# Gated cross-attention with a mixture of experts: the first group's steps issued ahead of all others

## The chip, the core and the metric

The kernel runs on one core of a Trainium2 chip. The time is device time in microseconds for one execution; the median over several runs is compared. The core has a matrix engine (PE), a vector engine (DVE), a scalar engine (ACT), a general engine (POOL) and a queue engine that mostly starts transfers (SP). ACT and POOL can start transfers too. Each engine takes its instructions in order; the engines wait for one another through semaphores.

## The reference, cut to what matters

```python
# x (64, 128, 128), context (64, 77, 96), mask (64, 77)
x = x + tanh(g_xattn[0]) * attention(layernorm(x), context, mask, Wq, Wk, Wv, Wo)
x = x + tanh(g_ffn[0]) * moe(layernorm(x), Wg, W11, W12, W2)

# attention: 16 heads of 8
q, k, v = x @ Wq, context @ Wk, context @ Wv          # split by heads
scores = where(mask, q @ k.T * 8**-0.5, -max)         # 128 x 77 for each head
out = (softmax(scores) @ v) @ Wo

# moe: 8 experts, the 2 best for each token
top, idx = top_k(softmax(x @ Wg), 2); top = top / (top.sum(-1) + 1e-8)
out = sum over the two of top * ((silu(x @ W11[e]) * (x @ W12[e])) @ W2[e])
```

All arrays are float32 but the mask.

## The kernel before, in words

**Tiling.** The 64 batches of 128 tokens are 16 groups of four (`G = 4`, `NG = 16`). A group has a tile of x (128 partitions x 4 x 128, 256 KB) that stays on the chip, a tile of context (77 x 4 x 96) and, in the attention part, keys, queries and values of its own. After the attention, tokens are sent by expert to a buffer in HBM in two parts (groups 0 to 11, and 12 to 15), worked on there in tiles of 128 rows, and brought back, added to x and stored.

**The mask.** `keep64` holds it as 64 x 77 numbers (L216). It is used in three ways: transposed by PE to `keepT`, from which `firstT` (the first kept position of each batch) and `drop` (what is added to a score's exponent) come; as `live` (L246), which zeroes the layer norm's factor of a batch with no position kept; and by rows: it is stored to `keep_d` in HBM (L218) and each group loads its four rows back, copied to all 77 partitions, as `kr` (L456). POOL makes from it a selection matrix `sel` (steps `sel_0`, `sel_1`, `sel_2`, L479 to L499) with which the context is multiplied while it is transposed.

**The steps of a group.** The attention of a group is cut into named steps: `loads` (x, context and `kr` on SP), `stats_a0` and `stats_a1` (mean and variance on DVE, then Ln and Exp on ACT and the product with `live` on POOL, L342 to L355), `shift_a` (L359, DVE), `rows_a0` and `rows_a1` (the normalized rows, ACT, L365), `queries_t` (four transposes on PE and a copy on ACT, `pt`), `queries` (`pq`, L543), `context_t` (`pc`, L505), `keys` (`pk`, L526, and four scaled copies `kb` on ACT, L532). Then come the batches, one in each turn: `scores` (`sc`, L840, four PE products; then on DVE the maximum `mx`, L849, and two differences `pe` and `pls`, L852), `turn` (eight transposes `tp`, L862, and exponentials on ACT, L867), `turn_last` (`tl`, L875), `values` (`pv`, L813 and L825, and a copy `va` on ACT, L831), `mix` (48 products `po`, L894). Later steps of the group (`inverses`, `quotients`, `project`, `residual` and the routing) follow some turns on.

**The order.** Inside the block that contains the attention the order on PE, ACT, DVE and POOL is the order in which the program issues the instructions; SP's loads stand in the order of the program and of their buffers. A table `AT` gives each step a turn relative to its group's first batch and whether it stands before (`PRE`) or after (`POST`) the turn's batch work. The main loop (L916) counts turns from -15; `advance` issues, in each half turn, the steps of all groups that fall due, so in the turns ahead of batch 0 the steps of groups 0, 1, 2 and 3 alternate. In turn i the scores of batch i, the transposes of batch i-1, the values of batch i+2 and the product of batch i-2 are issued.

**Buffers.** The scores have one PSUM tile of four banks (`ps_sc`), so a batch's scores wait for DVE to have read the last batch's. All other products share three PSUM tiles (`product`, L372): transposes, queries, keys, `po` and `tl` in turn. `values` writes one PSUM tile `pv`, read by `va`. Four context tiles and three `kr` tiles are in turn, so a later load waits until an earlier tile has been read. A transfer also waits for the transfer eight before it to have landed, since eight semaphores are used in turn.

**The start.** SP starts the mask and the context of group 0, ACT the x of group 0, then Wk, Wq, Wv, eight pieces of Wo (rows are permuted on the way, L129), Wg and the two gates (L133, L134). ACT makes `tg`, the tanh of the gates, with a table of its own, and then loads the table of Ln and Exp (L305, L307); DVE makes `wo` from `tg` and `wo_in` (L306) and then takes up the statistics.

Of the kernel before, what the change touches and what calls it, by code (L numbers as in the profile page):

```python
# [8 lines left out]
F32 = mybir.dt.float32  # L9
# [4 lines left out]
ALU = mybir.AluOpType  # L14
# [5 lines left out]
NQ = 4  # L20
HQ = HEADS // NQ
G = 4
# [14 lines left out]
def tile_gated_xattn_moe(  # L37
# [81 lines left out]
    nc.sync.dma_start(out=mask_u8, in_=mask)  # L119
    load_c(0)  # L120
    nc.scalar.dma_start(out=xs[0], in_=x[0:G].rearrange("b t d -> t b d"))
# [3 lines left out]

    for q in range(NQ):
        for k in range(2):
            r = 32 * q + 16 * k
            nc.scalar.dma_start(  # L129
                out=wo_in[r : r + 16], in_=Wo[32 * q + 16 * (1 - k) : 32 * q + 16 * (2 - k)]  # L130
            )
    nc.scalar.dma_start(out=wg, in_=Wg)
    nc.scalar.dma_start(out=gates[:, 0:1], in_=g_xattn.partition_broadcast(P))  # L133
    nc.scalar.dma_start(out=gates[:, 1:2], in_=g_ffn.partition_broadcast(P))  # L134
# [81 lines left out]
    nc.vector.tensor_scalar(keep64, mask_u8, none64, None, ALU.max)  # L216
    keep_d = tc.dram_tile([B, M], F32, name="keep_d")
    nc.sync.dma_start(out=keep_d[:, :], in_=keep64)  # L218
    keepT = const.tile([M, B], F32, name="keepT")
# [78 lines left out]
    with ExitStack() as ph:  # L298
# [7 lines left out]
        nc.vector.tensor_scalar_mul(wo, wo_in, tg[:, 0:1])  # L306
# [25 lines left out]
        class Norm:  # L332
# [12 lines left out]
            def factors(self, live=None, late=False):  # L345
# [8 lines left out]
                if live is not None:  # L354
                    nc.gpsimd.tensor_tensor(self.rs, self.rs, live, ALU.mult)  # L355
# [84 lines left out]

        def step(name):
            def add(f):
                TURN.setdefault(AT[name], []).append(f)
                return f

            return add
# [3 lines left out]
        def loads(gr, g):  # L450
# [4 lines left out]
            gr.kr = a3.tile([M, G, M], F32, tag="kr", name=f"kr_{g}")  # L455
            nc.sync.dma_start(out=gr.kr, in_=keep_d[b0 : b0 + G].partition_broadcast(M))  # L456
# [96 lines left out]
        def quotients(gr, g):  # L553
            gr.aT = s2.tile([P, T], F32, tag="aT", name=f"aT_{g}")
# [352 lines left out]
        groups = [Group() for _ in range(NG)]  # L907

        def advance(i, where):
# [5 lines left out]
        NBT = NG * G  # L915
        for i in range(min(TURN)[0], NBT + 2):  # L916
# [152 lines left out]
        while t < len(ts) + 6 or rest or any(k >= t for k in at):  # L1069
            tile_steps(t)  # L1070
            n0 = len(ts) if t >= parts[0].nt - 4 else parts[0].nt - 4 - t
            for f, g in [rest.pop(0) for _ in range(-(-len(rest) // n0))]:
                f(groups[g], g)
# [42 lines left out]
```

## Time and profile before

| | |
|---|---|
| median of 3 runs | 699.18 us (698.61 to 702.12) |
| the profiled execution | 720.7 us, of it the span 719.0 us |
| granted TensorE clock, mean | 0.98 |
| PE busy | 627.0 us (87%) |
| POOL, DVE, ACT busy | 442.2, 466.5, 394.5 us |
| chain that ended last, PE's share | 74% |
| first table load on ACT | 12.45 us |
| first scores on PE | 30.70 us |
| attention's end, first expert tiles | about 390 to 403 us |

The span is the time from the first to the last instruction of one execution under the profiler; the profiled execution is longer than the median of the runs. Times are from the span's start. A busy share is an average over parts of the program with different limits. In a line of the profile the engine comes first, then the line of the kernel, the operation, what is written and what it is read from; in brackets stands the idle time of the engine just before and what ended it.

### The profile page before, as it was taken

To read this page: it belongs to the slowest core of one execution; us is meant where nothing else is said; L and a number is where in the kernel's file an instruction comes from. 1 tells how busy PE (TensorE), PEld (TensorE's weight loads), DVE (VectorE), ACT (ScalarE), POOL (GpSimd) and SP (SyncE) were. 2 spreads that over 40 slices of the span, in tenths; PEclk is the share of its full clock that TensorE was granted. 3 is DMA by queue.
4 is the path that set the end of the run, shared out by engine and by line. 5 is a ranking of instruction groups with operands and counts; after the bars stand their busy time and mean duration, and the time that the engine had idled before them with its cause. 6 is when DMAs were issued, how large, how long until landed. Compare 5 with 4: busy or idle time off the path is not lost.

```text
span 719.0 us, 21356 instructions
## 1 busy us (share of the span) xinstructions
PE 627.0 (87%) x7695; PEld 433.6 (60%) x7695; DVE 466.5 (65%) x1437; ACT 394.5 (55%) x1042; POOL 442.2 (61%) x770
## 2 busy tenths in 40 slices
PE   2799999999999999998888699898989798999870
PEld 1477777777677777675666266455655465666450
DVE  3467898878878887876697345454455454555673
ACT  1768987787878877786645333443343232333220
POOL 4311113767566755755465487888778888887661
PEclk9999999999999999999999899999999999999995
DMA  6680000111110100000010332222222313253766
GB/s 163 178 227 15 15 10 25 33 38 37 32 37 30 36 26 24 29 26 24 29 55 25 80 101 67 75 69 71 65 70 68 102 58 87 75 188 105 200 191 199
DMA packets 64598, 53.65 MB, mean 75 GB/s; under 512 B 14142, under 2 KB 58323, under 8 KB 64496
## 3 DMA queue, kind: packets, MB, share of 16 engines
q1 hardware_dynamic: 45824, 30.54, 15.9%
q0 software_dynamic: 8640, 17.06, 7.3%
q10 hardware_dynamic: 10032, 4.69, 2.4%
q8 instruction: 63, 1.03, 0.6%
q14 instruction: 39, 0.32, 0.2%
HBM read 28.98 MB, written 24.20 MB: 74 GB/s over the span
## 4 chain that ended last, share of the span: by engine, by line
PE 74%; DVE 8%; ACT 6%; issue 5%; DMA 3%; POOL 1%; another core or an unknown queue 1%; SPq 0%; POOLq 0%; ACTq 0%; DVEq 0%
PE pu L982 17%; PE po L894 11%; PE tp L862 8%; PE pot L1005 7%; PE sc L840 6%; PE phh L997 4%; PE ptt L972 4%; PE tl L875 3%; PE pq L543 3%; PE pg L617 2%; PE py L564 2%; PE pv L813 2%; PE pc L505 2%; DVE mx L849 1%; DVE pe L852 1%
## 5 line engine op out<-in xcount | busy, mean ns | idle before, releaser
L1013 POOL DMA_INDIRECT yb<-y,xt x142 | 140.8, 992 | 53.4 <-DVE xTt L974 24.3
L702 POOL DMA_INDIRECT xg<-rows,dest x128 | 127.2, 993 | 68.0 <-DVE gm L624 43.6
L982 PE MATMUL pu<-wx,xTt 128*128 x284 | 154.3, 626 | 9.4 <-issue 9.0
L988 ACT ACTIVATE sgt<-pu 128x256 f32<-128x256 f32 x142 | 54.4, 383 | 175.4 <-PE pu L982 105.1
L990 DVE TENSOR_TENSOR ht<-sgt,pu 128x256 f32<-128x256 f32 x142 | 59.6, 420 | 101.2 <-ACT sgt L988 61.7
L849 DVE TENSOR_REDUCE mx<-sc 128x16 f32<-128x1232 f32 x64 | 91.6, 1431 | 29.2 <-PE sc L840 25.2
L867 ACT ACTIVATE pT<-tp,drop 128x512 f32<-128x512 f32 x128 | 80.3, 676 | 14.0 <-PE tp L862 11.6
L997 PEld LDWEIGHTS phh<-ident,ht 128*128 128x128 f32 x284 | 39.0, 142 | 81.2 <-issue 66.0
L1005 PE MATMUL pot<-wx,hTt 128*128 x568 | 87.5, 277 | 0.2 <-issue 0.2
L852 DVE TENSOR_TENSOR pe<-sc,mx 128x1024 f32<-128x1024 f32 x64 | 78.4, 1224 | 2.2
L1005 PEld LDWEIGHTS pot<-wx,hTt 128*128 128x128 f32 x568 | 75.4, 193 | 0.4 <-issue 0.4
L862 PEld LDWEIGHTS tp<-ident,pe 128*128 128x128 f32 x512 | 56.2, 143 | 28.4 <-issue 11.1
L894 PE MATMUL po<-pT,own 128*32 128x128 f32 x1536 | 65.6, 274 | 8.6 <-issue 8.6
L862 PE MATMUL tp<-ident,pe 128*128 128x128 f32 x512 | 71.7, 284 | 0.8 <-issue 0.4
L1011 DVE TENSOR_SCALAR y<-pot,xt 128x128 f32<-128x128 f32 x142 | 49.0, 346 | 32.3 <-PE pot L1005 12.9
L894 PE MATMUL po<-pT,va 128*32 128x128 f32 x1536 | 62.2, 274 | 2.9 <-issue 2.9
L355 POOL TENSOR_TENSOR rs_a<-rs_a,live 128x4 f32<-128x4 f32 x16 | 3.2, 199 | 98.9 <-ACT rs_a L353 94.5
L972 PE MATMUL ptt<-ident,xt 128*128 128x128 f32 x142 | 42.2, 297 | 23.6 <-DVE xTt L974 8.0
L999 ACT COPY hTt<-phh 128x256 f32<-128x256 f32 x142 | 52.3, 368 | 15.7 <-PE ptt L972 10.2
L997 PE MATMUL phh<-ident,ht 128*128 128x128 f32 x284 | 55.4, 277 | 2.8 <-ACT hTt L999 1.4
L894 PEld LDWEIGHTS po<-pT,own 128*32 128x32 f32 x1536 | 46.6, 110 | 17.0 <-issue 16.7
L840 PE MATMUL sc<-kb,qT 32*128 32x308 f32 x512 | 53.1, 485 | 3.5 <-DVE pls L852 3.4
(162 smaller groups left out, 1118.6 us busy)
## 6 DMA issues: line engine op xcount, KB each, us to landing
xt<-xg SPq DMA_DIRECT2D x142, 66.0 KB
ys<-yb SPq DMA_DIRECT2D x16, 512.0 KB
out_dram<-x ACTq DMA_DIRECT2D x16, 256.0 KB
x<-in_x_dram SPq DMA_DIRECT2D x15, 256.0 KB
yb<-y,xt POOLq DMA_INDIRECT x142
wx<-in_L_ffn_W_dram SPq DMA_DIRECT2D x2, 1024.0 KB
xg<-rows,dest POOLq DMA_INDIRECT x128
xg<-empty SPq DMA_DIRECT2D x30, 66.0 KB
```

The source lines that it names most:

```text
L702: i = nc.gpsimd.indirect_dma_start(out=part_of(g).xg[:, :], out_offset=bass.IndirectOffsetOnAxis(ap=gr.dest[:, k, b : b + 1], axis=0), in_ ...
L840: nc.tensor.matmul(sc[:, q, :W], gr.qT[r, b * S : (b + 1) * S], gr.kb[r, b].rearrange("p h j -> p (h j)"), start=True, stop=True,)
L849: nc.vector.tensor_reduce(mx[:, :, :, 0], sv, AX.X, ALU.max)
L852: nc.vector.tensor_tensor(dst[:, :, :, : j1 - j0], sv[:, :, :, j0:j1], mx.to_broadcast([P, NQ, HQ, j1 - j0]), ALU.subtract,)
L862: nc.tensor.transpose(tp[:, u, :], pe[:, q + u // 2, 2 * (u % 2) : 2 * (u % 2) + 2].rearrange("p h j -> p (h j)"), ident,)
L867: nc.scalar.activation(pT[:, 2 * q : 2 * q + 4], tp, AF.Exp, bias=drop[:, 0, i : i + 1], scale=scale)
L894: nc.tensor.matmul(po[32 * q : 32 * q + 32, v, :], w, pT[:, 2 * q + c if c < 2 else 8 + q // 2, :], start=(c == 0), stop=(c == 2),)
L972: nc.tensor.transpose(pt, ti.x[:, :D], ident)
L982: nc.tensor.matmul(pu.rearrange("p j i -> p (j i)"), ti.xT, wxf[:, bass.ds(ti.e, 2 * I)], start=True, stop=True,)
L997: nc.tensor.transpose(pt[:, c], ti.h[:, c], ident)
L1005: nc.tensor.matmul(po, ti.hT[:, c], wxf[:, bass.ds(ti.e + w, D)], start=(c == 0), stop=(c == NC - 1),)
L1013: i = nc.gpsimd.indirect_dma_start(out=ti.pt.yb[:, :], out_offset=bass.IndirectOffsetOnAxis(ap=ti.x[:, D : D + 1].bitcast(I32), axis=0), i ...
```

## The change

1. The two gates are loaded on SP, right behind the mask and the first context; the eight pieces of Wo and Wg go to SP too, behind the store of `keep_d`. ACT's queue holds only x of group 0, Wk, Wq and Wv, and x is asked for ahead of the context in the program.
2. Group 0's mask rows don't go through HBM: PE multiplies `keep64` by four matrices of zeros and a row of ones (`sel_b`), which copies row b to 77 partitions; the result is copied to `kr0`.
3. The product with `live` is on DVE for group 0, on POOL for all others.
4. `wo` is made in group 0's step `quotients`, not ahead of everything.
5. Steps are named in the table of turns and issued by `run`. A list `FIRST` is issued ahead of turn 0: all of group 0's steps up to its queries, loads of groups 1 and 2, group 0's context and keys, and the statistics and selection of group 1 and part of those of group 2. The loop begins at turn 0. The other steps of groups 1 and 2 have half turns of their own (`EARLY`): group 1's rows before the batch of turn 1, its context and transposes after it, its queries and keys after turn 2; group 2's rows in turn 2, context and transposes at the head of turn 3, queries after turn 3. All else that fell due before turn 0 is issued after turn 0's batch. Turn 0 issues the values of batches 0, 1 and 2.

```diff
     nc.sync.dma_start(out=mask_u8, in_=mask)
+    nc.scalar.dma_start(out=xs[0], in_=x[0:G].rearrange("b t d -> t b d"))
     load_c(0)
-    nc.scalar.dma_start(out=xs[0], in_=x[0:G].rearrange("b t d -> t b d"))
+    nc.sync.dma_start(out=gates[:, 0:1], in_=g_xattn.partition_broadcast(P))
+    nc.sync.dma_start(out=gates[:, 1:2], in_=g_ffn.partition_broadcast(P))
     nc.scalar.dma_start(out=wk, in_=Wk)
     nc.scalar.dma_start(out=wq, in_=Wq)
     nc.scalar.dma_start(out=wv, in_=Wv)
-
-    for q in range(NQ):
-        for k in range(2):
-            r = 32 * q + 16 * k
-            nc.scalar.dma_start(
-                out=wo_in[r : r + 16], in_=Wo[32 * q + 16 * (1 - k) : 32 * q + 16 * (2 - k)]
-            )
-    nc.scalar.dma_start(out=wg, in_=Wg)
-    nc.scalar.dma_start(out=gates[:, 0:1], in_=g_xattn.partition_broadcast(P))
-    nc.scalar.dma_start(out=gates[:, 1:2], in_=g_ffn.partition_broadcast(P))
...
+    sel_b = const.tile([B, G, M], F32, name="sel_b")
+    nc.vector.tensor_copy(
+        sel_b, ident[:B, :G].unsqueeze(2).to_broadcast([B, G, M])
+    )
     keep_d = tc.dram_tile([B, M], F32, name="keep_d")
     nc.sync.dma_start(out=keep_d[:, :], in_=keep64)
+
+    for q in range(NQ):
+        for k in range(2):
+            r = 32 * q + 16 * k
+            nc.sync.dma_start(
+                out=wo_in[r : r + 16], in_=Wo[32 * q + 16 * (1 - k) : 32 * q + 16 * (2 - k)]
+            )
+    nc.sync.dma_start(out=wg, in_=Wg)
...
+        pq0 = ps_m.tile([M, G, M], F32, name="pq0")
+        for b in range(G):
+            nc.tensor.matmul(pq0[:, b], sel_b[:, b], keep64, start=True, stop=True)
+        kr0 = const.tile([M, G, M], F32, name="kr0")
+        nc.vector.tensor_copy(kr0, pq0)
...
         nc.scalar.activation(tg, gates, AF.Tanh)
-        nc.vector.tensor_scalar_mul(wo, wo_in, tg[:, 0:1])
         nc.scalar.preload_act_table_set("natural_log_exp_and_others")
...
                 if live is not None:
-                    nc.gpsimd.tensor_tensor(self.rs, self.rs, live, ALU.mult)
+                    on = nc.vector if self.n == "a0" else nc.gpsimd
+                    on.tensor_tensor(self.rs, self.rs, live, ALU.mult)
...
-            gr.kr = a3.tile([M, G, M], F32, tag="kr", name=f"kr_{g}")
-            nc.sync.dma_start(out=gr.kr, in_=keep_d[b0 : b0 + G].partition_broadcast(M))
+            if g > 0:
+                gr.kr = a3.tile([M, G, M], F32, tag="kr", name=f"kr_{g}")
+                nc.sync.dma_start(
+                    out=gr.kr, in_=keep_d[b0 : b0 + G].partition_broadcast(M)
+                )
+            else:
+                gr.kr = kr0
...
         def quotients(gr, g):
+            if g == 0:
+                nc.vector.tensor_scalar_mul(wo, wo_in, tg[:, 0:1])
...
+        FIRST = [
+            (n, g)
+            for g, names in (
+                (0, "loads stats_a0 stats_a1 shift_a sel_0 sel_1 sel_2 rows_a0 rows_a1"),
+                (0, "queries_t queries"),
+                (1, "loads"),
+                (2, "loads"),
+                (0, "context_t keys"),
+                (1, "stats_a0 stats_a1 shift_a sel_0 sel_1 sel_2"),
+                (2, "stats_a0 sel_0 sel_1"),
+            )
+            for n in names.split()
+        ]
+        EARLY = {
+            (n, 1): 2 * i + where
+            for n, i, where in (
+                ("rows_a0", 1, PRE), ("rows_a1", 1, PRE), ("context_t", 1, POST),
+                ("queries_t", 1, POST), ("queries", 2, POST), ("keys", 2, POST),
+            )
+        }
+        EARLY["rows_a0", 2], EARLY["rows_a1", 2] = 4, 5
+        EARLY["context_t", 2], EARLY["queries_t", 2], EARLY["queries", 2] = 6, 6, 7
+        SCHED = {}
+        for h in range(2 * min(TURN)[0], 2 * (NBT + 3)):
+            for g in range(NG):
+                for n in TURN.get((h // 2 - G * g, h % 2), ()):
+                    if (n, g) not in FIRST:
+                        SCHED.setdefault(EARLY.get((n, g), max(h, 1)), []).append((n, g))
...
         def advance(i, where):
-            for g in range(NG):
-                for f in TURN.get((i - G * g, where), ()):
-                    f(groups[g], g)
+            run(SCHED.get(2 * i + where, ()))
...
-        for i in range(min(TURN)[0], NBT + 2):
+        run(FIRST)
+        for i in range(NBT + 2):
...
-            if 0 <= i + 2 < NBT:
-                g, b = divmod(i + 2, G)
-                vas[i + 2] = values(groups[g], g, b)
+            for j in range(0 if i == 0 else i + 2, min(i + 3, NBT)):
+                vas[j] = values(groups[j // G], j // G, j % G)
```

More of the change, by code (lines that the diff above doesn't have):

```diff
@@ L439, in tile_gated_xattn_moe @@
         TURN = {}
+        STEP = {}
         def step(name):
             def add(f):
-                TURN.setdefault(AT[name], []).append(f)
+                STEP[name] = f
+                TURN.setdefault(AT[name], []).append(name)
                 return f
@@ L907, in tile_gated_xattn_moe, with run @@
         groups = [Group() for _ in range(NG)]
+        NBT = NG * G
+        FIRST = [
[26 more added lines that the diff above has]
+                        SCHED.setdefault(EARLY.get((n, g), max(h, 1)), []).append((n, g))
+        def run(steps):
+            for n, g in steps:
+                STEP[n](groups[g], g)
         def advance(i, where):
-            for g in range(NG):
-                for f in TURN.get((i - G * g, where), ()):
-                    f(groups[g], g)
+            run(SCHED.get(2 * i + where, ()))
         pes, vas, pTs = {}, {}, {}
-        NBT = NG * G
-        for i in range(min(TURN)[0], NBT + 2):
+        run(FIRST)
+        for i in range(NBT + 2):
             advance(i, PRE)
@@ L1071, in tile_gated_xattn_moe @@
             n0 = len(ts) if t >= parts[0].nt - 4 else parts[0].nt - 4 - t
-            for f, g in [rest.pop(0) for _ in range(-(-len(rest) // n0))]:
-                f(groups[g], g)
+            run([rest.pop(0) for _ in range(-(-len(rest) // n0))])
             for f, g in at.get(t, ()):
```

## Prediction

> **What bounds the kernel now.** I read the page first: TensorE is busy 87% of the span, and the chain that ended last is 74% PE. From about 36 us to the end of the attention part PE hardly waits, so a change to the order at the start is worth what it moves the point where PE becomes full. I therefore took the busy time by windows:
>
> ```profile
> 0.00:10.00 10.00, 2.10 (x9) 1.82 (x9) 3.94 (x15) 0.00 (x0) 5.83 (x37) 1.00 0.52 138
> 10.00:20.00 10.00, 2.51 (x11) 1.90 (x11) 4.92 (x23) 4.77 (x9) 3.77 (x6) 1.00 0.70 170
> 20.00:30.00 10.00, 8.31 (x44) 4.58 (x43) 2.81 (x11) 6.92 (x21) 3.84 (x8) 1.00 0.50 130
> ...
> 40.00:50.00 10.00, 10.00 (x149) 7.09 (x151) 5.46 (x11) 5.77 (x15) 2.38 (x4) 1.00 0.89 229
> 50.00:60.00 10.00, 9.97 (x242) 7.55 (x231) 7.70 (x11) 9.32 (x24) 0.00 (x0) 1.00 0.18 52
> 60.00:70.00 10.00, 10.00 (x200) 7.50 (x199) 8.30 (x15) 7.95 (x21) 2.65 (x6) 1.00 0.09 25
> ```
>
> After the window's length the columns are PE, PEld, DVE, ACT, POOL. PE works 4.6 of the first 20 us and all of each window from 40 on. The waits of the first 36 us name the first stop:
>
> ```profile
> ACT L305 <- DMA gates<-in_g_xattn_dram: 12.5, 1, 12.5
> ...
> DVE wo L306 <- ACT tg L305: 5.5, 1, 5.5
> ```
>
> Then the order of time (start, duration, engine, line):
>
> ```profile
> 14.46 1.28 ACT L307 ACT_TABLE_LOAD   x1
> 14.47 0.29 DVE L306 TENSOR_SCALAR wo<-wo_in,tg 128x128 f32<-128x128 f32 x1 [5.49 <-ACT tg L305]
> ...
> 15.26 0.23 DVE L342 BATCH_NORM_STATS2 st_a<-x 128x6 f32<-128x128 f32 x1
> ...
> 18.50 1.65 ACT L365 ACTIVATE xn<-x,nm_a,rs_a 128x128 f32<-128x128 f32 x4 [0.98 <-DVE nm_a L359]
> ...
> 30.70 1.41 PE L840 MATMUL sc<-kb,qT 32*128 32x308 f32 x8
> ...
> 35.31 1.41 PE L840 MATMUL sc<-kb,qT 32*128 32x308 f32 x8 [1.31 <-DVE pls L852]
> ...
> 41.83 1.41 PE L840 MATMUL sc<-kb,qT 32*128 32x308 f32 x8
> ...
> 47.87 0.80 PE L840 MATMUL sc<-kb,qT 32*128 32x308 f32 x8
> ...
> 51.77 0.80 PE L840 MATMUL sc<-kb,qT 32*128 32x308 f32 x8
> ...
> 56.10 0.80 PE L840 MATMUL sc<-kb,qT 32*128 32x308 f32 x8
> ```
>
> The gates are last of eleven small loads on ACT's queue and land at 12.45 and 14.23. DVE's `wo` stands in front of the first statistics, so it holds group 0 although x0 is in by 3.96 (the second `c` load on SP, which waits for x0, issues then). Group 0's rows begin at 18.50, its first scores only at 30.70, because group 1's and 2's steps are interleaved. The scores at 56.10 (group 1's second batch) are my milestone: both orders have then done the same PE work.
>
> **The Trainium skill.** "ScalarE: Activation LUTs", What ACT_TABLE_LOAD costs, gives 1283 ns and about 1380 ns of drain per switch. The trace agrees on 1.28 us and shows no drain: `tg` ends at 14.43, the next load starts at 14.46. I charge 1.28. "TensorE: Matmul & The Clock Gate", Part 1, says matmuls run at half clock until a free-running window of about 3.4 us has been busy, and Part 4 that transposes don't count alike. Here score groups take 1.41 until 41.83 and 0.80 at 47.87; the durations change near 44.9, 9.6 us after the dense stretch begins at 35.31. Longer than the page says, but that stretch is partly transposes; I use 9.6. "DMA: Bandwidth & Descriptors", Anatomy of one DMA, gives about 2.0 us fixed; the gates here needed 3.33 and 3.52 from issue, and I use those. Its section Issuing engines are not separate DMA queues says that all issuers share 16 engines: moving loads between ACT and SP buys order, not bandwidth.
>
> **Part 1: gates early.** Issued third and fourth on SP (mask 0.82, c 1.46, so about 2.1 and 2.6), they land at 5.4 and 6.1. ACT: load 1.28, `tg` 0.20, load 1.28, ready at 8.2 against 15.74. On DVE `wo` leaves, `pv`'s memset goes ahead of the mask. From the mask at 4.2: `inv` 1.63, `none` 0.25, then four statistics pairs (1.55 for four at 15.26) with two mask operations between, 8.1. Ln and Exp (0.32 + 0.20) end at 8.7. A new wait: `keep64` now stands behind the first statistics, which wait for x0; behind it wait all mask work, `live` and the `keep_d` store. With x0 in by 3.96 it costs nothing; each microsecond of delay beyond 6.1 would go through. Meanwhile DVE has nine constants queued before `rs*live` (`sel_b`, `hm`, two `h`, `keepT`, `live`, `own` x4, 0.10 to 0.25 apart, so 0.9 to 2.2 in all; I take 1.7): 9.8. Were the drain real, ACT would be ready at 9.6 with the tables and nothing but 0.3 would change. The product with `live`, now on DVE, saves a hop to POOL; it and `nm` (0.15 to 0.64) end near 10.4. Rows at 10.5 instead of 18.50: 8.0 us.
>
> **Part 2: mask rows by TensorE.** Removed: group 0's `kr` load behind `keep_d` (issue 6.43, data used at 11.53). Added: `sel_b`, four 77x77 matmuls (like `pc`: 1.46), one copy (about 0.4, like `cT`). No row of before shows these; bounds: 0.7 us if the clock were full, 2 us if each waits for the copy of `sel_b`; I take 1.5. PE is idle at 7 to 10 us, which hides them; without that cover they cost that much. On DVE the copy and `firstT` stand after `nm`: 11.1. Then three `sel` steps on POOL, 2.37 from the row at 17.75: 13.5. `pc` is wanted at 15.4, so this costs nothing; two microseconds of cover.
>
> **Part 3: group 0 undivided.** Rows to the end of `pq` took 18.50 to 23.43 = 4.93: 15.4. Then `pc` 1.46, `cT` 0.39, `pk` 1.24, four `kb` 1.72, with hops: first scores at 20.3 against 30.70. Gain there 10.4.
>
> **Part 4: what was skipped comes back.** The turns before, between scores: 4.61, 6.52, 6.04, 3.90, 4.33 = 25.40. After, with the same rows:
> Turn 0: ACT's Ln and Exp of group 1 stand behind `kb`, then POOL, `nm` 0.64 and half of x2's statistics 0.8 stand on DVE before the first `mx`: 0.7 late, 5.3. Three `values` run inside DVE's 2.95.
> Turn 1: the PE list is the old one (sc, tp, pv, tl, pc, pt, with group 1 in place of 2): 6.5, with 0.3 for ACT, which has group 1's rows (1.65) in front of the exponentials: 6.8.
> Turn 2: old list, then `pk` 0.66, `pc` 0.66, `pt` 0.44, and 0.3 for group 2's second rows: 8.1.
> Turn 3: 3.90 plus `pq` 0.86, plus 0.4 because transposes need the PSUM slot that four `kb` (1.74) still read: 5.2.
> Turn 4: 4.4.
> Sum 29.8, so 4.4 back. Milestone at 50.1 against 56.10: **6.0 us earlier**. The dense stretch starts with the scores of turn 1 in both, so I let the clock rise at the same place; a window of 3.4 us either way moves this by up to 1.7.
>
> **Part 5: queues.** On SP, x1 now stands behind two gates, eight `wo_in` pieces (ACT took 5.83 for eight), `keep_d` and `wg`: about 11.4 against 2.08. x2 follows at 12.7. At some 215 GB/s, the rate at 3 to 6 us, the 0.72 MB up to x2 takes 3.4 plus the landing: x2 near 17, x3 near 19. Wanted: x1 and x2 by 22, x3 by 26. Hidden, with 5 us of cover. `wo` is wanted in turn 6, its 0.29 on DVE lies beside PE. Expert weights are issued near 31 as before and used first at about 400. `c` of group 5 now stands before x6, which is first used in turn 10. Beyond turn 5 the order per engine is the old one, and no wait from there on depends on the clock on the wall: dispatches, tile list and tiles follow PE and DVE.
>
> Against its own time: span 719.0, execution 720.7; 719.0 - 6.0 = 713.0. The runs' median is 699.18, 3% below the profiled one. I carry the difference over: **693.2 us**. If loads land sooner unprofiled, less is saved, perhaps 1 us.
>
> **Rivals.**
> A, most of the 10.4 stays: the extra preparation fits into PE's idle time in turns 0 to 1 and ACT's tail isn't waited for. For it: PE idles through part of DVE's 2.95 in turns 0 and 1. Against: turns 2 and 3 are solid. 9 to 10.5 saved: 689 to 690.
> B, given back: the dense stretch has more gaps, the clock stays half through turns 2 and 3 (`tp` 0.95, `po` about 1, `pq`, `pk`, `pc`, `pt` about 3 more), or ACT's serial copies rule turn 3. 3 to 5.5 lost: 696 to 699.
> C, slower: DVE is in order and x2's statistics stand before the first `mx`. If x2 lands late, every score waits. It decides from x2 landing at 22; no gain at 28; over 0.5% slower past 31.5. Price for 33: 11 late, 704. For it: ten more issues, each waiting for the load eight earlier; the x load issued at 12.81 took 4.76. Against: 12.7 + 4.76 is 17.5.
>
> **Numbers.** My forecast, 690.5 to 695.7, 0.62; A 0.14; B 0.15; C 0.09. Half a per cent, 3.5 us, is about what a measurement can tell from no change: faster needs below 695.7 (forecast and A, 0.76), slower above 702.7 (C, 0.09), between 0.15 (B). The range 688.0 to 698.5 takes A and nearly all of B.
>
> **What would show it.** First table load near 5.4; group 0's rows near 10.5; first scores near 20; first `mx` about 1 us after those scores end, and released by PE or DVE, not by x; turns 2 and 3 longer by 2.1 and 1.3; milestone near 50; score groups at 0.80 from turn 3 on. It is wrong if `mx` is released by a load of x (C), if turns 2 or 3 run at the slow durations (B), or if PE waits later for work that the early start made due sooner.

## The result, and the profile after

| | before | after |
|---|---|---|
| median of 4 runs each | 699.17 us (698.61 to 702.12) | 691.74 us (691.10 to 692.44) |
| ratio, 95% interval | | 0.9889 [0.9866, 0.9911] |
| the profiled execution, its span | 720.7, 719.0 us | 692.33, 690.2 us |
| PE busy | 627.0 us (87%) | 615.3 us (89%) |
| group 0's rows on ACT | 18.50 us | 9.53 us |
| first scores | 30.70 us | 20.05 us |
| milestone (second batch of group 1) | 56.10 us | 46.54 us |
| first expert tile | 403.07 us | 386.88 us |

The change saves 7.43 us (1.1%); 693.2 was forecast. The two spans are 28.8 us apart, and most of that is not the change: the profiled execution of before was an odd one, about 3% longer than its own runs, while that of after is one of its four runs. So it has to be asked what the 7.4 us are made of, and whether the sum that came close to them was right. Of the runs of the kernel before on another chip, used further down, one took 1448 us; the ratios leave it out.

The order of time after, lines picked from the engines' timelines (start, duration, engine, line; in brackets the idle time before and what ended it):

```profile
5.76 1.28 ACT L315 ACT_TABLE_LOAD   x1 [5.76 <-DMA gates<-in_g_ffn_dram]
...
7.28 1.28 ACT L316 ACT_TABLE_LOAD   x1
...
9.53 1.65 ACT L375 ACTIVATE xn<-x,nm_a,rs_a 128x128 f32<-128x128 f32 x4 [0.43 <-DVE nm_a L369]
...
14.87 1.46 PE L523 MATMUL pc<-sel,c 77*96 77x77 f32 x8
...
20.05 1.41 PE L860 MATMUL sc<-kb,qT 32*128 32x308 f32 x8 [1.83 <-ACT kb L550]
...
21.28 0.28 DVE L351 BATCH_NORM_STATS2 st_a<-x 128x6 f32<-128x128 f32 x1
...
22.09 1.41 DVE L869 TENSOR_REDUCE mx<-sc 128x16 f32<-128x1232 f32 x1
...
25.19 1.41 PE L860 MATMUL sc<-kb,qT 32*128 32x308 f32 x8 [0.72 <-DVE pls L872]
...
28.98 0.44 PE L895 MATMUL tl<-ident,pls 128*128 128x128 f32 x2
...
30.45 0.80 PE L860 MATMUL sc<-kb,qT 32*128 32x308 f32 x8
...
36.90 0.80 PE L860 MATMUL sc<-kb,qT 32*128 32x308 f32 x8
...
42.21 0.80 PE L860 MATMUL sc<-kb,qT 32*128 32x308 f32 x8
...
46.54 0.80 PE L860 MATMUL sc<-kb,qT 32*128 32x308 f32 x8
```

Three things are to be seen. The first table load waits for the gates until 5.76 and no longer until 12.45, and on PE and ACT group 0's chain runs from there to its scores with no step of another group between. The statistics of x2 at 21.28 have no bracket: they were not waiting for their load, and the first maximum follows at 22.09. And `tl` at 28.98 is already at the short duration, so PE works at full clock 3.8 us after the scores of turn 1, where before showed 9.6.

Busy time in windows of 10 us after (PE, PEld, DVE, ACT, POOL):

```profile
0.00:10.00 10.00, 2.65 (x15) 2.36 (x15) 6.10 (x27) 3.74 (x7) 5.14 (x36) 1.00 0.25 61
10.00:20.00 10.00, 6.56 (x20) 3.82 (x19) 2.01 (x10) 4.61 (x13) 2.22 (x3) 1.00 0.69 181
20.00:30.00 10.00, 8.03 (x131) 5.74 (x132) 8.89 (x21) 5.87 (x15) 4.76 (x8) 1.00 0.36 98
30.00:40.00 10.00, 9.43 (x168) 6.88 (x170) 6.34 (x12) 9.30 (x25) 4.61 (x7) 1.00 0.75 204
```

PE now works 9.2 of the first 20 us (4.6 before), and the third window has 131 matmul records instead of 44, since turns 0 and 1 now lie in it. What still idles on PE lies in the serial chain before 20 us and in turns 0 and 1.

### The profile page after: what moved, and what is told of

It is laid out like the page before. It is cut to its first block, busy times and chain, and to the rows that moved or that the text cites. A ratio compares the mean times of both kernels' runs of the same rounds, so it can differ in the third digit from the quotient of the medians.

```text
span 690.2 us, 21369 instructions
## 1 busy us (share of the span) xinstructions
PE 615.3 (89%) x7703; PEld 429.2 (62%) x7703; DVE 466.1 (68%) x1440; ACT 392.9 (57%) x1042; POOL 442.0 (64%) x769
## 4 chain that ended last, share of the span: by engine, by line
PE 71%; DVE 9%; ACT 6%; issue 5%; POOL 5%; DMA 3%; another core or an unknown queue 1%; POOLq 0%; ACTq 0%; DVEq 0%; SPq 0%
PE pu L1035 16%; PE po L914 11%; PE tp L882 8%; PE pot L1058 7%; PE sc L860 5%; PE phh L1050 4%; PE ptt L1025 3%; PE tl L895 3%; POOL yb L1066 3%; PE pq L561 3%; PE py L584 2%; PE pc L523 2%; PE pg L637 2%; PE pv L833 2%; DVE x L1101 2%
## 5 line engine op out<-in xcount | busy, mean ns | idle before, releaser
L914 PE MATMUL po<-pT,va 128*32 128x128 f32 x1536 | 60.8, 274 | 2.3 <-issue 2.0
L1035 PEld LDWEIGHTS pu<-wx,xTt 128*128 128x128 f32 x284 | 43.4, 193 | 19.0 <-issue 17.5
```

The costliest lines, as they stand in the source:

```text
L914: nc.tensor.matmul(po[32 * q : 32 * q + 32, v, :], w, pT[:, 2 * q + c if c < 2 else 8 + q // 2, :], start=(c == 0), stop=(c == 2),)
L1035: nc.tensor.matmul(pu.rearrange("p j i -> p (j i)"), ti.xT, wxf[:, bass.ds(ti.e, 2 * I)], start=True, stop=True,)
```

## Experiments

The theory: the whole gain is the earlier milestone; from there on it is a rigid shift. Its main part comes from group 0 no longer waiting, first for the gates and then for the other groups' steps. Rivals: the gates alone give it; the order alone gives it; the way through HBM was a stop; it is the TensorE clock, not the order, that made the difference between the two profiles.

### The two kernels again

No edit; the pair on other chips.

> The kernel before, unchanged, profiled a second time. The first profiled execution took 720.7 us beside runs of about 699. Theory: that execution was an odd one, with some 20 us lost here and there after 100 us, and this one has a span near 697, first scores near 30.7 and the scores of group 1's second batch near 56. Rival: the profile of this kernel is always longer than its runs, span near 719 again.

> The changed kernel again, beside the runs below, since chips differ by some per cent. Theory: the first profile of the kernel before had its clock rise late, by about one window (9.6 us into the dense stretch against 3.4 to 4.8 in all other profiles); the second one reaches the scores of group 1's second batch at 53.84, so the real lead is 53.84 - 46.54 = 7.3 us, and the whole gain is made there: 7 to 7.5 us below the kernel before on this chip, the scores at 46 to 47. Rival: the lead is 9.5 us and 2 are lost later: scores near 46.5 but a third profile of the attention's end showing less lead.

The kernel before took 660.92 us in one run (662.92 us median over that chip's runs), the kernel after 654.49 us (654.37 to 654.58, 4 runs) against 662.78 (660.23 to 665.68): 0.9885 [0.9858, 0.9913]. The two chips take the same for the kernel before, so their profiles can be laid side by side. Score groups of before, second profile:

```profile
30.63 1.41 PE L840 MATMUL sc<-kb,qT 32*128 32x308 f32 x8
...
35.23 1.41 PE L840 MATMUL sc<-kb,qT 32*128 32x308 f32 x8 [1.31 <-DVE pls L852]
...
40.94 0.80 PE L840 MATMUL sc<-kb,qT 32*128 32x308 f32 x8
...
45.60 0.80 PE L840 MATMUL sc<-kb,qT 32*128 32x308 f32 x8
...
53.84 0.80 PE L840 MATMUL sc<-kb,qT 32*128 32x308 f32 x8
```

Score groups and one group of transposes of after, second profile:

```profile
25.19 1.41 PE L860 MATMUL sc<-kb,qT 32*128 32x308 f32 x8 [0.71 <-DVE pls L872]
...
30.73 0.80 PE L860 MATMUL sc<-kb,qT 32*128 32x308 f32 x8
...
37.17 0.80 PE L860 MATMUL sc<-kb,qT 32*128 32x308 f32 x8
38.55 1.09 PE L882 MATMUL tp<-ident,pe 128*128 128x128 f32 x8 [0.57 <-ACT kb L550]
...
46.81 0.80 PE L860 MATMUL sc<-kb,qT 32*128 32x308 f32 x8
```

In this profile of before the clock rises some 4.8 us after the scores of turn 1, not 9.6, and the milestone is 53.84, not 56.10. In the second profile of after it rises 4.4 us after them. With clocks so nearly alike the account is:

| between scores | turn 0 | 1 | 2 | 3 | 4 | sum |
|---|---|---|---|---|---|---|
| before, second profile | 4.60 | 5.71 | 4.66 | 3.91 | 4.33 | 23.21 |
| after, second profile | 5.14 | 5.54 | 6.44 | 5.31 | 4.33 | 26.76 |
| longer by | 0.54 | -0.17 | 1.78 | 1.40 | 0.00 | 3.55 |
| predicted | 0.7 | 0.3 | 2.1 | 1.3 | 0.1 | 4.4 |

First scores 30.63 - 20.05 = 10.58 earlier, 3.55 given back, 7.03 left at the milestone. The -0.17 in turn 1 is the earlier rise, not the order. After that nothing is won or lost: the lead is 6.98 us at the last batch's scores (351.80 against 344.82), 7.17 at the first expert tile, 6.8 in the span. The medians differ by 8.3 us on these chips and by 7.4 and 7.3 where the kernel before takes 699 us; the part over 7 isn't accounted for by the profiles. The runs of before scatter more (5.4 us against 0.2 on the chip of the second profile of after). Each run has a mean granted clock on record: 0.980 to 0.981 in the four runs of after there, 0.958 to 0.980 in the eleven of before. So most runs of before were longer at the lower clock; how much of the difference this makes isn't shown, since on that chip none of them has a profile.

### The parts alone: gates, old order, late gates

`gates_only` is the kernel before with the gates on SP and `wo` moved:

```diff
     load_c(0)
     nc.scalar.dma_start(out=xs[0], in_=x[0:G].rearrange("b t d -> t b d"))
+    nc.sync.dma_start(out=gates[:, 0:1], in_=g_xattn.partition_broadcast(P))
+    nc.sync.dma_start(out=gates[:, 1:2], in_=g_ffn.partition_broadcast(P))
...
-    nc.scalar.dma_start(out=gates[:, 0:1], in_=g_xattn.partition_broadcast(P))
-    nc.scalar.dma_start(out=gates[:, 1:2], in_=g_ffn.partition_broadcast(P))
...
-        nc.vector.tensor_scalar_mul(wo, wo_in, tg[:, 0:1])
...
         def quotients(gr, g):
+            if g == 0:
+                nc.vector.tensor_scalar_mul(wo, wo_in, tg[:, 0:1])
```

> The kernel before with two edits: the gates third and fourth on SP, and wo made in group 0's step quotients. My theory: ACT's tables are ready near 8.5, but the context product of group 0 still waits for the mask rows through HBM until about 13.2 and stands ahead of group 0's transposes on TensorE, so these begin near 14.7 instead of 19.05: 4.3 us gained, 694.9. Rival, the gates are the whole cause: 691.7. Rival, the gates were not what held the start: 699.

`old_order` is the kernel after with the steps in their old turns; loads, mask rows and the product on DVE stay:

```diff
-        FIRST = [
...
-        EARLY["context_t", 2], EARLY["queries_t", 2], EARLY["queries", 2] = 6, 6, 7
+        FIRST = []
+        EARLY = {}
...
-        for i in range(NBT + 2):
+        for i in range(min(TURN)[0], NBT + 2):
...
-            for j in range(0 if i == 0 else i + 2, min(i + 3, NBT)):
+            for j in range(max(i + 2, 0), min(i + 3, NBT)):
```

> The changed kernel with its order of steps undone: FIRST and EARLY empty, the loop begins at turn -15 as before; gates first, mask rows by TensorE and the rest stay. My theory: group 0's factors again stand behind the first half of group 1's statistics, which wait for x1 (in at 13.8 in the changed kernel), so rows at about 14.7, first scores near 27, some 3.8 us of the gain left: 695.5 us. Rival: the early gates are all of the gain and the order is worth nothing: 691.7. Rival: the order is all of it: 699.

`late_gates` is the kernel after with the loads of before: gates last on ACT, `wo` made ahead of the statistics.

```diff
-    nc.sync.dma_start(out=gates[:, 0:1], in_=g_xattn.partition_broadcast(P))
-    nc.sync.dma_start(out=gates[:, 1:2], in_=g_ffn.partition_broadcast(P))
...
+    nc.scalar.dma_start(out=wg, in_=Wg)
+    nc.scalar.dma_start(out=gates[:, 0:1], in_=g_xattn.partition_broadcast(P))
+    nc.scalar.dma_start(out=gates[:, 1:2], in_=g_ffn.partition_broadcast(P))
...
         nc.scalar.activation(tg, gates, AF.Tanh)
+        nc.vector.tensor_scalar_mul(wo, wo_in, tg[:, 0:1])
```

> The changed kernel with the loads of the gates, Wo and Wg and the making of wo put back as before; order, mask rows by TensorE and the product with live on VectorE stay. My theory: tables and wo at 14.5 as before, rows near 17.7, first scores near 28.3, then the changed kernel's 26.5 us to the scores of group 1's second batch: 54.8 against 56.1, 1.3 us gained, 697.9. With the two runs above this says whether the parts add up (4 + 1.3 against 7.4) or need each other. Rival: order alone gives most of the gain, 693.

| | group 0's rows | first scores | milestone | ahead there | median, us | ratio to before |
|---|---|---|---|---|---|---|
| before, second profile | 18.43 | 30.63 | 53.84 | | 662.92 | |
| gates only | 14.23 | 26.43 | 49.50 | 4.34 | 659.53 (18 runs) | 0.9949 [0.9931, 0.9967] |
| old order | 14.83 | 27.03 | 50.45 | 3.39 | 657.59 (6 runs) | 0.9933 [0.9893, 0.9972] |
| late gates | 18.85 | 28.75 | 55.01 | -1.17 | 665.78 (12 runs) | 1.0031 [0.9999, 1.0064] |
| all together | 9.51 | 20.05 | 46.81 | 7.03 | 654.49 (4 runs) | 0.9885 [0.9858, 0.9913] |

The parts don't add: 4.34 - 1.17 is 3.2, all together is 7.0. The early gates alone bring a good half, as was expected, though in another way: ACT's tables were ready only at 11.50, not near 8.5, because ACT first issues the eight pieces of Wo (until 8.20). It cost nothing, since group 0's transposes wait for `pc`, from 13.42 to 14.78. The new order alone was expected to bring a little over 1 us at the milestone, and in its one profile loses as much.

Milestones and medians don't rank the parts alike: by the median the gates alone bring 3.4 us and the old order with all the new loads 5.3, by the milestone 4.3 and 3.4. The two intervals overlap, and something comes between. In the profile of the gates alone the lead is 4.29 at the last scores, 3.97 at the first expert tile, 2.1 some ten microseconds later, 1.3 at PE's last product and nothing at the end (spans 659.4 and 659.2). The largest piece of this goes where the expert tiles begin: PE stays at half clock there for 10.24 us instead of 3.41 (see the last section). The profile of late gates has the same. Its twelve runs fall apart accordingly: five of 660.9 to 664.1 us with a mean granted clock of 0.978 to 0.981, seven of 665.5 to 669.3 with 0.933 to 0.974. So the rigid shift holds for the pair of profiles above, not for every execution, and that late gates are slower than before isn't shown by the medians (the interval takes in 1).

Up to the milestone the timelines say why the parts don't add. Old order with early gates:

```profile
12.68 1.56 PE L523 MATMUL pc<-sel,c 77*96 77x77 f32 x8 [1.92 <-POOL sel L517]
...
13.84 0.29 DVE L351 BATCH_NORM_STATS2 st_a<-x 128x6 f32<-128x128 f32 x1 [2.75 <-DMA x<-in_x_dram]
...
14.83 1.65 ACT L375 ACTIVATE xn<-x,nm_a,rs_a 128x128 f32<-128x128 f32 x4 [6.03 <-DVE nm_a L369]
...
27.03 1.41 PE L860 MATMUL sc<-kb,qT 32*128 32x308 f32 x8
```

ACT is ready and stands 6.03 us for DVE's `nm` of group 0; DVE has half of group 1's statistics in front of it, which wait for x1. This wait is made by the change's own loads. The eight pieces of Wo now stand on SP ahead of x1, which is issued near 10.9. In the kernel before it is issued at 2.08, and with the gates alone, where Wo stays on ACT, at 3.93; there group 1's statistics begin at 7.80 and wait for nothing:

```profile
3.93 0.39 SPq L99 DMA_DIRECT2D x<-in_x_dram  x1
...
7.80 0.26 DVE L341 BATCH_NORM_STATS2 st_a<-x 128x6 f32<-128x128 f32 x1
```

So the old order with all the new loads has its first scores 0.6 us later than the gates alone; the other 0.35 at the milestone is turn 1, where the clock rose 0.7 us later. Late gates with the new order:

```profile
11.95 1.28 ACT L315 ACT_TABLE_LOAD   x1 [11.95 <-DMA gates<-in_g_xattn_dram]
...
18.85 1.65 ACT L376 ACTIVATE xn<-x,nm_a,rs_a 128x128 f32<-128x128 f32 x4 [0.43 <-DVE nm_a L370]
...
28.75 1.41 PE L859 MATMUL sc<-kb,qT 32*128 32x308 f32 x8 [1.83 <-ACT kb L551]
```

Here the order takes only 1.9 us off the way to the first scores, because in the old order the other groups' preparation ran while group 0 waited for the gates. What was skipped then comes back in turns 0, 2 and 3, 26.26 us from first scores to milestone against 23.21. A little gained and three lost: in these profiles the order pays only once group 0 can start early.

### The second wait: x1 asked for earlier, old order

The old order again, with x1 issued right behind Wv, ahead of the pieces of Wo.

```diff
     nc.scalar.dma_start(out=wv, in_=Wv)
+    load_x(1)
...
             if g > 0:
-                load_x(g)
+                if g > 1:
+                    load_x(g)
```

> The run old_order (new start, old order of steps) with x1's load put ahead of the Wo pieces on SP. There group 0's factors ended at 14.7 because half of group 1's statistics stands before them and x1 came at 13.8. Theory: rows now at about 10.2; but in the old order the context product, at 12.7, stands ahead of group 0's transposes on TensorE, which begin near 14.2 instead of 15.4: 1.1 us earlier than old_order, scores near 25.9, about 5 us below the kernel before. So x1 is only the first of two waits that the old order has. Rival: x1 is the only one: rows at 10.2, scores near 22.5.

Old order, x1 early:

```profile
11.94 1.65 ACT L376 ACTIVATE xn<-x,nm_a,rs_a 128x128 f32<-128x128 f32 x4 [2.98 <-DVE nm_a L370]
12.71 1.56 PE L525 MATMUL pc<-sel,c 77*96 77x77 f32 x8 [1.93 <-POOL sel L519]
...
25.15 1.41 PE L862 MATMUL sc<-kb,qT 32*128 32x308 f32 x8
```

The rows come 2.9 us earlier and the first scores 1.9, so the wait for x1 was real. The rows were expected near 10.2; ACT still stands 2.98 us for `nm`, which on DVE has half of group 1's statistics, the copy of the mask rows, `firstT` and `drop` in front of it, and `pc` stands ahead of group 0's transposes at 14.07, as expected. The median, 694.64 us (693.14 to 696.02, 4 runs), is 0.9911 [0.9882, 0.9941] of the kernel before on that chip (699.78), and after in the same set took 692.51. By the medians that is 5.1 of 7.3 us; the old order without the earlier x1 gave 5.3 of 8.3 on the other chips. So the 1.9 us at the first scores can't be seen in the median. In this profile the clock rose only 9.0 us after the scores of turn 1, and the milestone (50.34) is no earlier than with x1 late (50.45); whether the other runs had it so late too isn't known. What is shown is the wait, not that taking it away pays without the new order.

### The mask rows through HBM again

Group 0's rows of the mask are loaded from `keep_d`, behind its store, in place of the four products and the copy.

```diff
     nc.sync.dma_start(out=keep_d[:, :], in_=keep64)
+    kr0 = const.tile([M, G, M], F32, name="kr0")
+    nc.sync.dma_start(out=kr0, in_=keep_d[0:G].partition_broadcast(M))
...
-        pq0 = ps_m.tile([M, G, M], F32, name="pq0")
-        for b in range(G):
-            nc.tensor.matmul(pq0[:, b], sel_b[:, b], keep64, start=True, stop=True)
-        kr0 = const.tile([M, G, M], F32, name="kr0")
-        nc.vector.tensor_copy(kr0, pq0)
```

> The changed kernel with part 2 undone: group 0's mask rows go through HBM again, stored and loaded back among the Wo pieces on SP; sel_b, its four products and the copy are gone. My theory (part 2 has about two microseconds of cover): the rows land near 11.6 to 12.5, the selection is done near 14 and the context product is asked for at 14.9: the same time within 0.5 us. Rival: the later loads of groups 1 and 2 or a late selection hold the first scores: 1 to 3 us slower.

The selection on POOL and the context products on PE, mask rows through HBM:

```profile
11.52 0.83 POOL L502 TENSOR_TENSOR sel<-sel,kr 77x308 f32<-77x308 f32 x1 [1.35 <-DMA kr<-keep_d]
...
14.95 1.45 PE L516 MATMUL pc<-sel,c 77*96 77x77 f32 x8
```

POOL waits 1.35 us for the load, and `pc` starts 0.08 later than with the products on PE (14.87), as do the first scores (20.13). The selection is done at 13.13 (12.62 with the products), well before `pc` is wanted: the cover is there, and in this kernel this part of the change is worth nothing on the path. The median, 655.84 us (654.55 to 658.60), 0.9902 [0.9865, 0.9939], is 1.3 us above after's with overlapping ranges; the profiled run, 658.6 us, is the longest of the five; in it the clock rose about 9.7 us after the scores of turn 1, and PE stayed at half clock for 10.24 us where the expert tiles begin.

### x1 and x2 late

Twenty-eight small loads of a piece of Wo, unused, stand on SP ahead of x1.

```diff
     nc.sync.dma_start(out=wg, in_=Wg)
+    junk = const.tile([16, 28, D], F32, name="junk")
+    for k in range(28):
+        nc.sync.dma_start(out=junk[:, k], in_=Wo[0:16])
```

> The changed kernel with 28 more loads of 8 KB on SP in front of group 1's and 2's loads, about 0.48 us each at issue, whose data isn't used. It puts x1 and x2 some 13.5 us later: x1 lands near 27.3, x2 near 29. My third rival of the prediction said that the first maximum then waits for x2 from 22 on: first maximum near 30.5 instead of 22.1, some 8 us lost, about as slow as the kernel before. Rival: the small loads pass at a higher rate than the Wo pieces, or the loss is made good in turns 2 and 3, which have other waits: under 4 us lost.

DVE and PE with x1 and x2 late:

```profile
26.92 0.29 DVE L354 BATCH_NORM_STATS2 st_a<-x 128x6 f32<-128x128 f32 x1 [15.83 <-DMA x<-in_x_dram]
...
30.87 1.41 DVE L872 TENSOR_REDUCE mx<-sc 128x16 f32<-128x1232 f32 x1
...
33.96 1.41 PE L863 MATMUL sc<-kb,qT 32*128 32x308 f32 x8 [2.50 <-DVE pls L875]
```

The first scores are where they were (20.06), but their maximum waits on DVE, which waits for x1: the first maximum comes 8.8 us later, the milestone 11.0, and the run takes 667.50 us (666.77 to 668.53), 1.0084 [1.0053, 1.0115] of before, where about the same as before was expected. The other 2.2 us at the milestone are turns 1 and 2 (6.52 and 7.67), at a clock that rose later. Some 2 us more appear only after the first expert tile (11.05 behind there, 13.2 at the last). Of these, 1.7 come in the first ten microseconds of the expert tiles, at half clock: the last column but two is the granted clock, first here, then in the second profile of after, each 3 to 4 us behind its first expert tile:

```profile
375.00:380.00 5.00, 4.75 (x9) 1.89 (x8) 2.27 (x11) 1.48 (x5) 1.06 (x5) 0.50 0.37 83
...
365.00:370.00 5.00, 4.52 (x19) 2.52 (x20) 2.02 (x7) 2.37 (x9) 1.40 (x5) 1.00 0.34 74
```

So rival C was a real way to lose: the order itself holds no cover, all of it lies in x1 and x2 arriving early (x1 by 13.80 in the kernel after).

The Trainium skill, "DMA: Bandwidth & Descriptors", Issuing engines are not separate DMA queues, says that a second issuing engine saves only the issuing time, "usually small relative to the DMA itself". In this place it isn't small: the 28 issues took 12.92 us of SP, 0.46 each, for pieces of 8 KB, and it was this that made x1 late: it was issued at 23.88 instead of 10.89.

### The clock: idle products

Three kernels put unused products on PE to make the clock rise earlier. `warm_pe` has four products (eight passes in the profile) at the very start:

```diff
+        warm = const.tile([P, 256], F32, name="warm")
+        nc.vector.memset(warm, 1.0)
+        pw = ps_m.tile([P, 256], F32, name="pw")
+        for k in range(4):
+            nc.tensor.matmul(pw, warm[:, :P], warm, start=True, stop=True)
         pk = ps_m.tile([M, B], F32, name="pk")
```

> The changed kernel with four more products of 128 x 256 ones on TensorE ahead of the mask's products, about 1.0 us each at half clock, from about 1.7 to 6 us, where TensorE has nothing to do; their result isn't used. Theory: the clock rises after one busy window, near 6 us, and stays if the gaps up to 20 us are short: pq 2.08 to about 1.0, pc 1.46 to 0.8, pk 1.39 to 0.7, scores 1.41 to 0.8, tp 1.97 to 1.1: 3 to 4 us faster than the changed kernel. Rival: the gaps between 6 and 20 us let the clock fall again, or the window isn't filled: within 0.5 us of the changed kernel.

They ran from 1.26 to 5.04 and nothing is seen of them: `pq` at 13.00 still takes 2.07, the first scores start at 20.05, the milestone is 47.12; 655.86 us (654.00 to 659.39), 0.9914 [0.9883, 0.9945], against 654.49 for after with overlapping intervals. This doesn't show that idle products can't raise the clock; the last section says why these may have been too short.

`fill_pe` puts nine 128x128 products of `ones` into PE's gaps from 12 to 23 us, and `fill_stats` also takes the first half of x2's statistics away from in front of the first maximum:

```diff
+        def fill(n, to=None):
+            for k in range(n):
+                nc.tensor.matmul(
+                    pv[:, 384:512] if to is None else to, ones, ones, start=True, stop=True
+                )
...
             gr.xT = transposed(gr.xn, f"a{g}")
+            if g == 0:
+                fill(1)
...
                 vas[j] = values(groups[j // G], j // G, j % G)
+                if i == 0:
+                    fill(1 + (j == 2), idle)
```

> The changed kernel with nine idle products of ones (128 x 128) on TensorE in the gaps between 12 and 25 us: one after group 0's transposes, one after its context product, three after its keys, one after each of the first two values and two after the third; their results are not used. Theory (the clock rises after a window of dense work wherever that comes): dense from about 11.2, so the slow durations end between 15 and 19 instead of near 29: scores of turn 1 and their transposes 0.6 and 0.9 shorter, scores of turn 2 near 28.7 instead of 30.7, 2 us faster than the changed kernel, and up to 4 where its window falls late. Rival: products of ones or transposes don't count, or the wait for VectorE's first maximum rules until 25 and the gain is under 0.5 us.

> As the run before, and the first half of group 2's statistics taken out of the list ahead of turn 0, so that it is issued behind the first batch's maximum on VectorE. Theory: the first maximum starts at 21.4 to 21.5 instead of 22.1, and what is put off still ends before the second maximum's scores are read, so 0.3 to 0.7 us more. Rival: it only moves VectorE's wait to the second maximum: no difference.

> The changed kernel once more, as the yardstick for the two runs below, which move it by less than a chip does. All theories: 1.1 to 1.2% below the kernel before on this chip, scores of group 1's second batch between 46.5 and 49.5 as the clock's window falls.

PE with the gaps filled:

```profile
14.80 0.83 PE L529 MATMUL pc<-sel,c 77*96 77x77 f32 x8
...
18.75 0.80 PE L872 MATMUL sc<-kb,qT 32*128 32x308 f32 x8 [1.17 <-ACT kb L560]
```

PE with the gaps filled and x2's statistics later:

```profile
14.89 1.45 PE L529 MATMUL pc<-sel,c 77*96 77x77 f32 x8
...
20.07 1.41 PE L872 MATMUL sc<-kb,qT 32*128 32x308 f32 x8 [0.56 <-ACT kb L560]
...
25.70 1.41 PE L872 MATMUL sc<-kb,qT 32*128 32x308 f32 x8
```

With the same products in the same places the clock rose at 14.7 us in one profile and at 30.6 in the other. Where it rose, the milestone came at 44.66, 2.2 us ahead of the unchanged kernel's 46.86 in the same set; where it didn't, the slow products didn't fit into the gaps and turn 0 grew from 5.14 to 5.63. In the first maximum the statistics gained what was expected (21.55 against 22.09) and no time came of it. The medians: 691.67 us (690.72 to 692.41) and 693.54 (693.18 to 693.97) beside 692.51 (692.15 to 694.25) for after, that is, 0.9871 [0.9844, 0.9898], 0.9901 [0.9878, 0.9923] and 0.9892 [0.9868, 0.9915] of before. Neither is shown to be better. Besides, the 2.2 us didn't last: the lead is 2.0 at 310 us, 1.6 at the last scores, 0.9 at the first expert tile and nothing at the end. What takes it away wasn't found.

## Why the prediction was right, and where it wasn't

**Part 1, gates early: right.** The table load began at 5.76 (5.4 predicted), the rows at 9.53 (10.5). Two steps were priced too high: DVE's nine constants, 1.3 for 1.7, and `nm`, which took 0.16. The drain that I left out isn't seen here either: the second load starts at 7.28, where `tg` ends at 7.25. The 2.0 us that the prediction quotes for a transfer stand in a section on those that the general engine starts, and the gates are started by ACT and SP; nothing in the sum rests on them.

**Part 2, mask rows on PE: right, and worth nothing.** The products took 1.32 (1.5 predicted), and the kernel with the rows through HBM loses 0.08 us on the path. The step was costed at nothing with about two microseconds of cover; that is what was found.

**Part 3: right in the sum, by two errors that cancel.** First scores 20.05 for 20.3. But the rows were 0.97 early, and from the rows to the scores it took 10.52 where 9.8 was forecast. The forecast took this leg from before, where the transposes begin 0.55 after the first row. In after PE works for the mask until 10.76 and starts them at 11.23, when all four rows are done, so the early rows bought almost nothing: with the mask rows through HBM the rows come at 10.23 and the first scores at 20.13. The trace puts the last 0.47 down to the rows, that of `warm_pe` to `drop` on DVE; which it is stays open.

**Part 4, what comes back: the mechanism right, the size off in two places that by luck nearly cancel.** The steps named for each turn are those that came: `nm` and x2's statistics in front of the first maximum (0.54 for 0.7), `pk`, `pc` and `pt` in turn 2 (1.78 for 2.1), `pq` and the wait of `tp` for `kb` in turn 3 (1.40 for 1.3, the wait 0.57 for 0.4). The term that was mis-sized is the one that I took from a single example: the clock rising 9.6 us after the dense stretch begins. It was 3.7 in the first profile of after, 4.4 in its second and 4.8 in the second of before. So turns 0 to 4 of after took 26.49 where 29.8 was forecast, the milestone was 46.54 and not 50.1; but the milestone of before that I subtracted from was late for the same reason, 56.10 where another execution has 53.84. With like clocks the lead is 7.03; I had 6.0. The 1.0 that is missing is 0.2 at the first scores and 0.85 in the turns, of which 0.17 is the clock's.

**Part 5, queues: right.** x1 was issued at 10.89 (11.4 predicted) and its statistics began at 13.80, x2 at 12.32 (12.7); no score waited for either. That this cover is needed is shown by the kernel with x late.

**The base: wrong in its reading, harmless in its use.** I took the profiled execution's 3% over the runs for a cost of being profiled and carried it over. After's profiled execution isn't longer than its other runs. The forecast took a difference inside one execution and put it on the median, so the odd base did no more than shift the milestone.

**Rivals.** A (most of the 10.4 stays) fails on turns 2 and 3: 3.55 came back. B (given back through slow turns) was the wrong way round in the profiles of after. It is what happens in some executions: with the mask rows through HBM, turns 1 to 3 took 6.52, 7.93 and 5.31. C didn't come, but its price was at least what I gave it: a first maximum 8.8 us late cost 11.0 at the milestone. And one case was not among my rivals: that the order would be worth nothing without the gates, and the gates little over half without the order. I had summed them as if the parts were separate steps of one path, which holds for the two together but not for either alone. Part 5 asked of the new order alone whether x1 comes in time behind the pieces of Wo; in the old one it holds group 0's rows.

## What to carry to other kernels

A load moved to another queue delays what stands behind it there: here the pieces of Wo put x1 nearly 9 us later, and in the old order an in-order engine then stood 6 us for it. So when parts of a change are tested one by one, ask of each whether it makes a wait that another part takes away. A reordering alone moves preparation out of time that was idle anyway into time that is full, so cost it with the stop still there before giving it a share of the gain. Take a clock's rise from more than one profile, and subtract two milestones only where both have it at the same place.

## What the runs showed of the hardware

**The clock's rise has two places.** Counted from the scores of turn 1, where PE becomes dense, it came after 3.1 to 5.2 us in eight of the twelve profiles without filled gaps, and after 9.0 to 9.7 in four (the first of before, the early x1, the late x1, the mask rows through HBM). Up to the rise the column of the granted clock says 1.00, because the trace's record of that clock begins only there; the half speed is seen in the durations alone. The Trainium skill, "TensorE: Matmul & The Clock Gate", Part 1, gives a free-running window of about 3.4 us, which would make the rise depend on where in the window the work begins. The traces agree. From the rise on, each recorded stretch of full or half clock but the last lasts a whole multiple of 3.41 us (354.99 is 104 windows; the short ones are 3.41, 6.83 and 10.24).

Count the same windows back from the rise, which is an estimate. In the eight early profiles a window began between 0.3 us before the scores of turn 1 and 1.8 after them, and the clock rose at its end. In the four late ones a window began 2.2 to 2.9 us after them; PE was busy all through it by the profile, and still the clock rose only at the end of the next. The early windows hold at least six of the eight transposes `tp` of turn 1, the late ones at most four, and else `pv`, `tl`, `pc` and `pt`. A window that began 0.3 us before the scores, with PE busy in 91% of it, raised the clock (late gates); one that began 0.5 before, at 85%, didn't (mask rows through HBM). So the place of the windows decides in these profiles, and busy alone isn't enough; what PE's work is measured by isn't shown. In `warm_pe` the windows so counted end at 2.9 and 6.3, and the 3.78 us of unbroken products from 1.26 to 5.04 fill neither.

**The clock falls once more where the expert tiles begin,** behind a gap in PE's work (in the second profile of after PE is busy 1.37 of the 5 us from 355 on). It stays at half for 3.41 us in both second profiles and for 10.24 in four others (gates only, late gates, late x1, mask rows through HBM). In each of these four the run falls 1.7 to 1.9 us further behind there, so between single runs a difference under 2 us says little about a change at the start.

**The same program takes 654.5 us on one chip and 692.5 on another,** with the same granted clock (0.98). From 86 us on eight turns take 41.6 us on the first and 43.7 to 45.9 on the second. The weight loads of one product between 130 and 300 us (busy time and mean of one, then the idle time before them and its releaser), on the slower chip:

```profile
L914 PEld LDWEIGHTS po<-pT,own 128*32 128x32 f32 x720 | 22.0, 109 | 11.5 <-issue 11.5
```

and on the faster:

```profile
L914 PEld LDWEIGHTS po<-pT,own 128*32 128x32 f32 x792 | 22.3, 110 | 0.0
```

The operations take the same; on the slower chip the loading of weights stops for 11.5 us ahead of them, for nothing that the profile names. Why, no run here shows.
